# Moving weight-term work, constant loads and an input load between chunks of a time-mix and GELU kernel

## Chip, cores and metric

The kernel runs on one core of one Trainium2 chip. The metric is the device time of one execution in microseconds (us). Before the change the median of three runs is 881.1 us (880.5 to 881.29).

## What is computed

The reference takes x of 4 x 1024 x 512 (float32). With `xn = layernorm(x)` it computes

```
xs  = xn one step earlier in time (the first step takes the second)
k   = (xn + (xs - xn) * time_mix_k) @ Wk.T       # 704 columns
r   = (xn + (xs - xn) * time_mix_r) @ Wr.T
s_t = s_(t-1) * exp(-exp(time_decay)) + relu(k_t)
a   = layernorm((s * r) @ Wv.T) * gamma + beta
d   = gelu(f16(xn) @ W0.T + bias0)               # 2048 columns, rounded to f16
e   = f16(d @ W1.T + bias1)
out = x + a + e
```

## The kernel before

**Tiling.** The 4096 tokens are eight blocks of 512 (`TB`). A block is done in 16 chunks (`for n in range(NN)`, line 964), one for each 128 of the 2048 inner columns of the feed-forward part. Chunk n issues the up product of chunk n+2 (`up`, L790, tile `pd`; from chunk 14 on that of the next block), then the down product of chunk n (`down`, L812, into four PSUM banks `pe`), then at most one piece of the time-mix part, which has tokens in the free dimension: a product for k or r in the early chunks, output products (`out_piece`: `out_full` L686 with `out_halves` L698, or `out_three_pass`) in chunks 12 to 15. What follows a piece (its eviction, the scan) is a generator run in the next chunk.

**Exactness by terms.** Weights and inputs are split into terms, which the products add up. W0 and W1 are split in two (`split`, lines 168 to 170: ScalarE casts the high term `hi`, VectorE subtracts). W1's terms, tile `w`, are made from a raw load `w1raw` in block 0, stored to DRAM and loaded from there in later blocks; it has two buffers, so that the split of chunk n+2 comes after the down product of chunk n. For k and r block 0 uses raw float32 weights in slow float32 products (`raw_k`, `raw_r`, L387; the last 64 hidden columns in `raw_halves`, tile `pkr`, L604); later blocks use `three_pass` with three terms for each weight tile (k or r, h of 0 to 4): L630 with two terms into bank `pa`, L387 with the third into bank `pb`, then ScalarE evicts `a` (L642) and VectorE adds `y` (L643). Each of those ten weight tiles gets its terms in `split_kr` (line 238): on VectorE a mask `wu` (L235), a difference `wd` (L243) and the third term (L247), on ScalarE two casts (L245, L246), and three stores to DRAM put on the list `stores`. `fetch_kr` (line 883) calls `load_kr`, three loads of 256 KB, for a later use. The tag `kr` has six buffers, two sets of terms.

**Order.** All instructions of TensorE, VectorE, ScalarE and SyncE inside the loop are in an order written out by hand (`manual_schedule`): each engine runs its own in this order and waits for semaphores. In a chunk the order is: up product, gelu of it (L800) and a cast (L805), down product, W1 load of later blocks (`load_w1`, L221), the piece's products, in block 0 the next raw W1 load (L208), then the jobs that `put(n, ...)` has hung on chunk n, in the order of the puts, woven with what follows the last piece; at the end, in block 0, the split of W1 for chunk n+2, and `store_weights`, which empties `stores` (L204). All loads and stores in the loop go through the one SP queue.

**Background jobs that the change touches.**
- `split_kr` in block 0: k's tile h in chunk 1 + 2h, r's in chunks 1, 3, 5, 7, 11.
- `load_late_constants` (lines 155 to 164) in chunk 4 of block 0: five loads of 256 KB and two of 128 KB for `wvraw` (the value weights, first used by `out_full` in chunk 12) and three broadcast loads (gamma, beta, bias1).
- In block 1: `fetch_x` (`load_x` of block 2, four loads) in chunk 2; its statistics (`stats`, L305 and L306) in chunks 4 and 5, `norm_apply` (L309) in chunk 6, and 16 transposes (`turn`, L331) in chunks 6 to 9 as 1, 6, 6, 3. `store_w0l` of group g in chunk 2g (four stores of 256 KB each); `split_wv` (three terms of `wvraw`, for blocks 2 on) of tile h in chunks 9, 11, 11, 12, 13, 13; r's `fetch_kr` for h of 2 to 4 in chunks 7 to 9.

**Buffers.** Products of the time-mix part and `pd` share four PSUM banks in turn (`ps_mm`). Tiles named by `temp` share six buffers. The tag `x` has one buffer: the x of the next block, and `xres`, in which the block's output is summed up and from which it is stored (`finish`, L775, store at L779; in the first two chunks of the block after). Most 128x512 tiles share 62 buffers of the tag `q`.

## Time and profile before

| | |
|---|---|
| median of three runs | 881.1 us (880.5 to 881.29) |
| the profiled execution: time, span | 882.43 us, 880.6 us |
| granted TensorE clock, mean | 0.991 |
| busy, share of the span | TensorE 98%, VectorE 76%, ScalarE 49%, GpSimd 8% |
| chain that ended last, by engine | TensorE 93%, DMA 3%, VectorE 3%, issue 1% |
| DMA | 198.95 MB, 226 GB/s over the span |
| block 0 of the profiled execution | first down product at 40.54 us, last chunk's at 134.16 us |
| block 1 | first down product at 143.33 us |

The profile is of one execution. PE is TensorE's matmuls, PEld its weight loads, DVE VectorE, ACT ScalarE, POOL GpSimd, SP SyncE; SPq is SP's queue of DMA issues. A timeline row holds start, duration, engine, line, operation, output and inputs without their numbers, and in brackets the idle time before it and what ended that. A row of waits holds total, number and longest. A row of stretches holds the stretch, its length, each engine's busy time with the number of instructions, the granted TensorE clock (1.00 is full), the share of time that the DMA engines were busy, and GB/s. L170 is line 170 of the kernel.

### The profile page before, as it was taken

Reading aid. Unit: us, or ns where it says so; the run is one execution under the profiler, and the core shown is the slowest. Engines: PE = TensorE matmul, PEld = TensorE weight load, DVE = VectorE, ACT = ScalarE, POOL = GpSimd, SP = SyncE. Lnnn points to the kernel's source line nnn. Section 1 sums busy time; section 2 is a strip of 40 time slices with the busy share of each in tenths; the row PEclk is TensorE's granted clock in tenths of the full one; section 3 lists DMA queues with packets and bytes.
Section 4 is the critical chain, followed back from the end, with each engine's and each line's share of the span. In section 5 each row is a group of like instructions: output and inputs, shape, how many; then the busy total and the mean of one; then the engine's idle time right before and its main releaser. Section 6 shows DMA issues by size and latency. Waiting matters only on the chain.

```text
span 880.6 us, 11149 instructions
## 1 busy us (share of the span) xinstructions
PE 863.9 (98%) x3760; PEld 688.5 (78%) x3760; DVE 670.4 (76%) x1098; ACT 431.9 (49%) x733; POOL 73.9 (8%) x142
## 2 busy tenths in 40 slices
PE   8999899999999999999999999999999999999996
PEld 7676557888578888888888888888888888888885
DVE  4777986687868878779786788878886887864547
ACT  3855662437525465344644447344553446444430
POOL 1100000000002002000011000200011200200001
PEclk8999999999999999999999999999999999999998
DMA  8579874985559565776559675595656956577631
GB/s 261 207 249 331 298 256 136 339 269 187 160 184 326 203 211 173 254 270 228 178 179 313 217 248 187 178 329 202 220 192 217 310 208 222 175 242 270 235 123 49
DMA packets 102325, 198.95 MB, mean 226 GB/s; under 512 B 11231, under 2 KB 25596, under 8 KB 102268
## 3 DMA queue, kind: packets, MB, share of 16 engines
q1 hardware_dynamic: 102208, 198.22, 67.0%
q8 instruction: 30, 0.49, 0.2%
q14 instruction: 27, 0.22, 0.1%
q10 hardware_dynamic: 60, 0.02, 0.0%
HBM read 169.36 MB, written 28.84 MB: 225 GB/s over the span
## 4 chain that ended last, share of the span: by engine, by line
PE 93%; DMA 3%; DVE 3%; issue 1%; SPq 0%; ACT 0%; DVEq 0%; ACTq 0%
PE pd L790 25%; PE pe L812 24%; PE pa L630 14%; PE pb L387 7%; PE oa L727 6%; PE po L686 4%; PE ob L735 3%; PE ph L659 3%; PE pk L387 2%; PE ob L737 1%; DMA w0raw<-in_L_ffn_W 1%; PE pr L387 1%; DMA wvraw<-in_L_attn_Wv 1%; PE pkr L604 0%; PE po L698 0%
## 5 line engine op out<-in xcount | busy, mean ns | idle before, releaser
L812 PE MATMUL pe<-w,d 128*128 128x512 f32 x1008 | 250.5, 391 | 4.9 <-DVE w L170 3.1
L812 PEld LDWEIGHTS pe<-w,d 128*128 128x128 f32 x1008 | 189.5, 188 | 45.6 <-DVE w L170 4.0
L790 PE MATMUL pd<-xf,w0h 128*128 128x512 f32 x512 | 203.5, 398 | 0.0
L790 PE MATMUL pd<-xf,w0l 128*128 128x512 f32 x512 | 199.3, 389 | 0.0
L800 ACT ACTIVATE d<-pd,late_sb 128x512 f16<-128x512 f32 x128 | 87.9, 687 | 161.7 <-PE pd L790 161.4
L790 PEld LDWEIGHTS pd<-xf,w0h 128*128 128x128 f32 x512 | 96.1, 188 | 25.9 <-issue 4.9
L790 PEld LDWEIGHTS pd<-xf,w0l 128*128 128x128 f32 x512 | 96.1, 188 | 21.7 <-issue 1.9
L643 DVE SCALAR_TENSOR_TENSOR y<-pb,a 128x512 f32<-128x512 f32 x70 | 48.4, 691 | 75.3 <-PE pb L387 74.4
L642 ACT ACTIVATE a<-pa 128x512 f32<-128x512 f32 x70 | 42.0, 600 | 91.1 <-PE pa L630 91.1
L805 ACT CAST d<-d 128x512 fp32r<-128x512 f16 x128 | 79.5, 621 | 4.1
L331 DVE STREAM_TRANSPOSE xnT<-x 32x512 f32<-32x512 f32 x112 | 78.6, 702 | 2.1
L630 PE MATMUL pa<-hk,kr 128*128 128x512 f32 x140 | 54.5, 389 | 0.0
L630 PE MATMUL pa<-lk,kr 128*128 128x512 f32 x140 | 54.5, 389 | 0.0
L630 PE MATMUL pa<-hr,kr 128*128 128x512 f32 x140 | 54.5, 389 | 0.0
L630 PE MATMUL pa<-lr,kr 128*128 128x512 f32 x140 | 54.5, 389 | 0.0
L299 POOL TENSOR_SCALAR ry<-mvy 128x1 f32<-128x1 f32 x32 | 16.5, 516 | 438.2 <-DVE mvy L306 438.2
L727 PE MATMUL oa<-wv,hg 128*128 128x512 f32 x120 | 46.7, 389 | 0.0
L727 PE MATMUL oa<-wv,lg 128*128 128x512 f32 x120 | 46.7, 389 | 0.0
L645 ACT ACTIVATE y<-y 128x512 f32<-128x512 f32 x35 | 22.2, 633 | 39.7 <-DVE y L643 39.7
L387 PE MATMUL pb<-mk,kr 128*128 128x512 f32 x140 | 37.4, 389 | 0.0
L387 PE MATMUL pb<-mr,kr 128*128 128x512 f32 x140 | 37.4, 389 | 0.0
L686 PE MATMUL po<-wvraw,g 128*128 128x512 f32 x80 | 35.6, 592 | 0.0
(160 smaller groups left out, 1312.4 us busy)
## 6 DMA issues: line engine op xcount, KB each, us to landing
w<-w1d SPq DMA_DIRECT2D x110, 512.0 KB, 3.6
kr<-krd SPq DMA_DIRECT2D x210, 256.0 KB, 4.8
w0l<-w0d SPq DMA_DIRECT2D x96, 256.0 KB, 4.0
x<-in_L_attn_x SPq DMA_DIRECT2D x32, 256.0 KB, 5.8
w1d<-w SPq DMA_DIRECT2D x16, 512.0 KB, 3.4
xres<-in_L_attn_x SPq DMA_DIRECT2D x32, 256.0 KB, 5.2
krd<-wt SPq DMA_DIRECT2D x30, 256.0 KB, 4.6
out<-xres SPq DMA_DIRECT2D x28, 256.0 KB, 4.9
```

The costliest lines, as they stand in the source:

```text
L331: nc.vector.transpose(dst[i * Q : (i + 1) * Q, :, :, j, :], src[j * Q : (j + 1) * Q, :, :, i, :],)
L387: return nc.tensor.matmul(dst, w[:, c, :], src, start=(c == 0), stop=(c == NC - 1))
L630: nc.tensor.matmul(pa, w[p][:, c, :], xs[j, c][p], start=(c == 0 and p == 0), stop=(c == NC - 1 and p == 1),)
L642: nc.scalar.activation(a, pa, AF.Copy, scale=1.0 + 1.0 / S)
L643: nc.vector.scalar_tensor_tensor(y, pb, -1.0 / S, a, ALU.mult, ALU.add)
L659: nc.tensor.matmul(pa, w[:, c].rearrange("p two k -> p (two k)"), xs[j, c][p], start=(c == 0 and p == 0), stop=(c == NC - 1 and p == 1),)
L686: nc.tensor.matmul(pos[s], gs[i, h][:, s * P : (s + 1) * P], wv_raw[h], start=(h == 0), stop=False,)
L727: nc.tensor.matmul(pa, gs[i, h][p][:, cols], wv[h][p], start=(h == 0 and p == 0), stop=(h == NF - 1 and p == 1),)
L790: nc.tensor.matmul(pd, w, xf[c], start=(c == 0 and p == 0), stop=(c == NC - 1 and p == 1),)
L800: nc.scalar.activation(d16, pd, AF.Gelu, bias=b0_sb[:, n : n + 1])
L805: nc.scalar.copy(d, d16)
L812: nc.tensor.matmul(pe[s] if sum_ is None else sum_, d[:, s * P : (s + 1) * P], w1[p][:, cols], start=(n == first and p == 0), stop=(n == e ...
```

## The change

In block 0, `split_kr` runs for k's five tiles in chunks 0, 1, 3, 5, 7 and for r's tiles 0 and 1 in chunks 0 and 7. The constants' loads stand in chunk 9. The splits of r's tiles 2, 3 and 4 stand in block 1, in chunks 8, 9 and 10, where `fetch_kr` calls `split_kr` if the raw weight is still there; the terms are used from SBUF in the chunk after, in place of being loaded, and are stored for later blocks. In block 1, x of block 2 is loaded in chunk 1, its statistics stand in chunks 2 and 3, its normalization in chunk 4, the transposes in chunks 6 to 9 as 4, 6, 4, 2. `store_w0l` of group g stands in chunk 4g, `split_wv` in chunks 11, 12, 13, 13, 13, 15. TensorE's instructions stay the same in number and order.

```diff
-    def split_kr(kind, h):
+    def split_kr(block, kind, h):
...
             def fetch_kr(block, kind, h):
-                ks[block, kind, h] = load_kr(block, kind, h)
+                fetch = split_kr if (kind, h) in raw_w else load_kr
+                ks[block, kind, h] = fetch(block, kind, h)
...
+                put(0, several, split_kr, (1, 0, 0), (1, 1, 0))
                 put(0, several, split_w0, (1, 2), (1, 3))
...
-                for h in range(NF):
-                    put(1 + 2 * h, split_kr, 0, h)
-                    put((1, 3, 5, 7, 11)[h], split_kr, 1, h)
+                for n, *which in ((1, 0, 1), (3, 0, 2), (5, 0, 3), (7, 0, 4), (7, 1, 1)):
+                    put(n, split_kr, 1, *which)
...
-                put(4, load_late_constants)
+                put(9, load_late_constants)
...
                     if k > 1:
-                        put(k - 2 + 2 * (k > 6), fetch_kr, i, kind, h)
+                        split_here = (kind, h) in raw_w
+                        put(k - 2 + 2 * (k > 6) + split_here, fetch_kr, i, kind, h)
...
-                    put(2, fetch_x)
+                    put(1 if i == 1 else 2, fetch_x)
                     for s in range(NS):
-                        put(4 + s // 2 if i == 1 else 4, stats, s)
-                    put(6 if i == 1 else 5, lambda: norm_apply(j, state["x"]))
-                    turns = (1, 6, 6, 3) if i == 1 else (4, 5, 4, 3)
+                        put(2 + s // 2 if i == 1 else 4, stats, s)
+                    put(4 if i == 1 else 5, lambda: norm_apply(j, state["x"]))
+                    turns = (4, 6, 4, 2) if i == 1 else (4, 5, 4, 3)
...
                 for g in range(NN // G):
-                    put(2 * g, store_w0l, g)
-                for h, n in enumerate((9, 11, 11, 12, 13, 13)):
+                    put(4 * g, store_w0l, g)
+                for h, n in enumerate((11, 12, 13, 13, 13, 15)):
                     put(n, split_wv, h)
```

## Prediction

> **What bounds the kernel now.** I read the page's first two parts, then the waits of TensorE, then the timeline of each engine where TensorE stands still. TensorE is busy for 863.9 of 880.6 us, so a change can win only the gaps. After the first 40 us there are three, all in front of the down product (L812), and all for one thing: the split second weight, `w`.

> ```profile
> PE 863.9 (98%) x3760; PEld 688.5 (78%) x3760; DVE 670.4 (76%) x1098; ACT 431.9 (49%) x733; POOL 73.9 (8%) x142
> ...
> PE pe L812 <- DVE w L170: 3.1, 2, 2.4
> PE pe L812 <- ACT w L169: 1.9, 1, 1.9
> ```

> The timeline of TensorE places them in the first block: in chunk 7 (down product due at 76.53, goes on at 77.40) and in chunk 9 (due at 88.01, first matmul at 90.03, second at 92.88).

> ```profile
> 76.30 0.39 PE L812 MATMUL pe<-w,d 128*128 128x512 f32 x1
> 77.40 1.89 PE L812 MATMUL pe<-w,d 128*128 128x512 f32 x7 [0.71 <-DVE w L170]
> 79.13 0.59 PE L387 MATMUL pr<-xr,wr 128*128 128x512 f32 x1
> ...
> 90.03 0.50 PE L812 MATMUL pe<-w,d 128*128 128x512 f32 x1 [1.85 <-ACT w L169]
> 92.88 2.86 PE L812 MATMUL pe<-w,d 128*128 128x512 f32 x7 [2.35 <-DVE w L170]
> ```

> The gaps cost more than their length: busy time by stretch shows the granted clock (column PEclk) down after the second one.

> ```profile
> 76.30:79.13 2.83, 2.12 (x10) 1.43 (x9) 2.73 (x4) 0.14 (x1) 0.57 (x1) 1.00 1.04 329
> 88.01:95.68 7.67, 3.47 (x10) 1.96 (x9) 7.49 (x12) 4.61 (x8) 0.00 (x0) 0.86 1.03 397
> 95.68:99.85 4.17, 4.17 (x33) 1.26 (x33) 4.03 (x7) 1.87 (x3) 0.00 (x0) 0.85 0.98 346
> ```

> Why is `w` late? ScalarE's and SyncE's timelines: ScalarE sits 5.10 us before the split of chunk 8's `w`, for a load issued at 75.25, behind ten constants' loads on the one SP queue (67.66 to 73.96). VectorE, late in its turn, then still does two weight splits and five transposes ahead of chunk 9's `w` (84.84 to 92.13).

> ```profile
> 67.66 2.38 SPq L159 DMA_DIRECT2D wvraw<-in_L_attn_Wv  x5
> 70.08 1.21 SPq L161 DMA_DIRECT2D wvraw<-in_L_attn_Wv  x2
> 75.25 0.33 SPq L208 DMA_DIRECT2D w1raw<-in_L_ffn_W  x1
> ...
> 81.53 0.62 ACT L169 CAST w<-w1raw 128x512 fp32r<-128x512 f32 x1 [5.10 <-DMA w1raw<-in_L_ffn_W]
> ...
> 88.54 3.57 DVE L331 STREAM_TRANSPOSE xnT<-x 32x512 f32<-32x512 f32 x5
> 92.13 0.69 DVE L170 TENSOR_TENSOR w<-w1raw,w 128x512 fp32r<-128x512 f32 x1
> ```

> [...] full clock up to 88.01, 0.86 and 0.85 in the two stretches after, 1.00 from 99.85. [...] the load that ScalarE awaited also delayed the gelu behind it (82.06), and below a wait of VectorE holds all behind it. [...] what stands behind a waiting issue waits too.

> **The change, part by part.** Times are on the old trace's clock.

> *Splits of k and r (`split_kr`).* One costs VectorE 0.46 + 0.72 + 0.61 = 1.8 us (start to start, 84.84 to 86.63), ScalarE two instructions of 0.62 and 0.63, and SP three stores of 256 KB. Chunk 0 gets two, where VectorE idles for 5.47 us (37.2 to 42.69); chunks 1, 3 and 5 keep one of two; chunk 7 keeps two; chunks 9 and 11 lose theirs; three go to the second block. In the built program's order the first two VectorE instructions of chunk 0 even move ahead of the first scans. That is 1.1 us, but the chain they lengthen ends in `w0l`, needed near 36, at about 34.4: free. ScalarE's four extra casts put chunk 1's gelu 1.9 us later (46.3 for 44.43), its result needed at 54.87: free.

> *The constants' loads leave chunk 4.* The load for chunk 8's `w` then goes out right after the store of chunk 6's, near 66.5, and lands near 71 (4.3 us for its like at 66.30, by the trace's semaphore records, from which all landings here are), long before ScalarE wants it (74.5).

> *First block, walked again.* Without the wait and with a split less in chunks 3 and 5, chunk 7's `w` leaves VectorE near 74.0, needed at 76.53: the first gap goes (79.13 - 76.30 = 2.83 us for a stretch that takes 1.82 elsewhere: 1.0 us). Chunk 8's `w` is done at 76.4, needed at 83.4. Chunk 9's is the tight one: the gelu of chunk 7 starts at 76.56 (its matmuls' end), the `w0l` behind it on VectorE ends 2.5 us later (82.06 to 84.84 less 0.28 of DMA wait), near 79.1; then the two splits and five transposes and `w` take 84.84 to 92.82 = 8.0 us: 87.1. TensorE, 1.0 us earlier, needs it at 87.2. So the second gap goes, with nothing to spare; a gap of 0 to 0.5 stays possible, and I count 0.1. What goes with it: 7.67 - 1.82 = 5.85 us up to 95.68, and in the next stretch (`pkr`) 4.17 less 4 x 0.86 = 3.44 at full clock (a float32 128x512 product takes 3.43 us for four): 0.73. Sum: 1.0 + 5.85 + 0.73 = 7.6, less 0.1.

> *The loads in chunk 9.* They stand behind chunk 10's `w1` store (VectorE near 89.5), so go out from 90.5 on. The program's waits hold the later ones to earlier landings; the seven of `wv` land by 100.6 if they take as long as in chunk 4 (10.1 us from the first issue to the last landing). The first user is chunk 12's output product, at 111.04 - 7.6 = 103.4: 3 us of cover. Behind them on SP stands the load of chunk 13's `w1`, held to about 98 and landed by 104; ScalarE comes to it near 103, TensorE at 109.6. Free, but if the cover went, each us late is a us of TensorE.

> *Three splits in the second block* (chunks 8 to 10, three stores and no load each; nine loads fewer). VectorE has the room: three transposes leave chunks 8 and 9 for chunk 6, and a `wv` split leaves chunk 9. The terms are used a chunk later; I find each done 4 us or more ahead. The `wv` splits move to chunks 11 to 15: three in chunk 13 end near 232, those ahead of the next block 4 us before their use. The `w0l` stores move from chunks 2, 4, 6 to 4, 8, 12: their old places are the stretch with DMA share 0.99 (145 to 175), so this eases it. All counted at nothing.

> *x of block 2 a chunk sooner: a new wait.* The load now stands at the end of chunk 1 and overwrites the tile whose last two output stores were issued at 154.31.

> ```profile
> 154.31 1.22 SPq L779 DMA_DIRECT2D out<-xres  x2
> 155.63 2.24 SPq L278 DMA_DIRECT2D kr<-krd  x3
> 158.03 0.32 SPq L221 DMA_DIRECT2D w<-w1d  x1
> ...
> 161.25 1.89 SPq L106 DMA_DIRECT2D x<-in_L_attn_x  x4
> ...
> 158.25 0.69 DVE L288 SCALAR_TENSOR_TENSOR mr<-lr,ur 128x512 fp32r<-128x512 f32 x1
> 160.83 0.69 DVE L643 SCALAR_TENSOR_TENSOR y<-pb,a 128x512 f32<-128x512 f32 x1 [1.89 <-PE pb L387]
> ```

> These stores landed at 160.17 and 160.82. So x goes out at 160.9, not at 158, 0.35 us sooner than before; with the least latency of its like (4.1) it lands near 165.0, with that of before (5.4) at 166.3. But its statistics moved two chunks, from 171.54 to 158.9, ahead of chunk 2's eviction `y` (160.83). VectorE thus waits some 6 us; two statistics take 1.7, `y` 0.7: it ends at 167.4 for a landing at 165.0. That `y` frees the PSUM bank which chunk 4's up product takes, at 167.07: a gap of 0.4 us, up to 1.7 for 166.3, none below 164.6. I take 0.4. Further on VectorE needs 6.0 us for each next eviction, TensorE gives 6.3: no second gap. On SP the load of chunk 4's `w` waits behind x: out at 162.9, landed by 167.5, needed at 168.88; `kr` of chunk 4 by 169.5, needed at 170.69. Both pass with 1.2 us or more.

> *Sum:* 7.6 - 0.1 - 0.4 = 7.1 us won. The profiled execution took 882.43 us (its span 880.6 and 1.8 around it): 875.3. The median of the runs shown is 881.1, 1.3 below; I take the same saving: 874.0.

> **The rivals.**
> - *VectorE keeps a gap in chunk 9 (or x lands at the slow end).* For it: 0.1 us of slack, and VectorE 98% busy in 88 to 95.7. Against it: a short gap loses no clock. Together 1 to 3 us less: 875 to 877.5.
> - *The second block's wait grows.* For it: DMA share 0.99 there, landings of 6 us and over. If x lands at 168 to 170, the gap is 3.4 to 5.4, and the clock may drop as in chunk 9 (1 to 1.5 us): 877.5 to 880.5.
> - *The saving is only moved.* The ten loads delay chunk 12's product or the `w1` loads behind them as they did in chunk 4. For it: they queue on SP again. Against it: 3 us of cover, and half the weight stores of before. It would give about 881.
> - *Slower: VectorE's wait for x in chunk 2 of the second block eats more than all.* Price: each us of landing past 164.6 is one of TensorE, and SP's `w` and `kr` behind x follow. It decides from a landing near 171 (7.1 us with 1 of clock is break-even at 170.7); 883 at 172.5. For that x must take 11 us; the longest load in this trace took 7.3.

> **How the numbers follow.** Forecast (873 to 875) 0.62; the first rival 0.22; the second 0.08; only moved 0.04; slower 0.04. The range, 872.8 to 878.0, leaves out most of the last three, and reaches below by run spread and a block-1 gap of nothing. A measurement can tell about 0.2% (1.8 us) from no change. Faster by more 0.90, within 0.05, slower 0.05.

> **What would show it.** Right: no gap of TensorE between 42 and 100, PEclk 1.00 there, ScalarE's wait for `w1raw` gone, the up product after `pkr` near 92.4 in place of 99.85, one wait of VectorE for x of 5 to 7 us in the second block with a gap under 2 us. Wrong: a gap at chunk 9 with the clock down after it, a wait of L686 for `wvraw`, or TensorE waiting for `y` again and again through the second block.

## The result, and the profile after

The changed kernel takes 874.17 us (median of 4 executions, 873.40 to 874.42), the kernel before, on the same chip, 881.19 us (4 executions, 880.50 to 881.64): the ratio is 0.992, with a 95% interval of 0.9902 to 0.9937. The forecast was 874.0 us, with a range of 872.8 to 878.0.

The profiled execution took 874.32 us. From its page:

```profile
span 872.5 us, 11125 instructions
PE 861.3 (99%) x3760; PEld 687.6 (79%) x3760; DVE 669.7 (77%) x1098; ACT 431.1 (49%) x733; POOL 73.8 (8%) x142
...
L812 PE MATMUL pe<-w,d 128*128 128x512 f32 x1008 | 248.9, 389 | 0.0
```

The down product (L812) now waits for nothing (last column: 0.0 us), and the waits of TensorE from 36 us on are an empty list. VectorE and ScalarE are as busy as before (669.7 and 431.1 us, against 670.4 and 431.9): beside nine loads of 256 KB, nothing was taken away but waiting. The timeline of TensorE shows the places where the gaps were (start, duration):

```profile
75.63 1.98 PE L812 MATMUL pe<-w,d 128*128 128x512 f32 x8
77.45 3.59 PE L387 MATMUL pr<-xr,wr 128*128 128x512 f32 x8
82.71 1.98 PE L812 MATMUL pe<-w,d 128*128 128x512 f32 x8
86.33 2.00 PE L812 MATMUL pe<-w,d 128*128 128x512 f32 x8
...
91.86 0.50 PE L790 MATMUL pd<-xf,w0h 128*128 128x512 f32 x1
```

And busy time by stretch shows the three stretches that the prediction priced, from the down product of chunk 7, from that of chunk 9, and the `pkr` products after it (stretch, length, busy PE, PEld, DVE, ACT, POOL; then PEclk, DMA share, GB/s):

```profile
75.63:77.45 1.82, 1.82 (x10) 1.50 (x8) 0.46 (x1) 1.52 (x3) 0.00 (x0) 1.00 1.00 279
86.33:88.14 1.81, 1.81 (x9) 1.26 (x7) 1.78 (x4) 1.31 (x2) 0.00 (x0) 1.00 0.53 210
88.14:91.86 3.72, 3.72 (x33) 1.13 (x33) 3.62 (x6) 0.62 (x1) 0.00 (x0) 1.00 0.90 274
```

They were 2.83, 7.67 and 4.17 us long, with the clock at 0.86 and 0.85 in the last two. Now they are 1.82, 1.81 and 3.72 at full clock: 1.01 + 5.86 + 0.45 = 7.3 us.

The spans differ by 8.1 us, the medians by 7.0. A part of that is the start. Ahead of the first down product of the first block TensorE has the same instructions in every kernel here (VectorE's order differs a little), yet that product starts at 40.54 us in the profile of before, at 39.91 in that of after, and between 38.88 and 40.54 in all profiles of this study. From it to the end, the kernel before takes 880.6 - 40.54 = 840.06 us and the changed one 872.5 - 39.91 = 832.59: the change is worth 7.47 us by one profile of each. Below I call this the span from the first down product; it compares single profiles to about 0.1 us (three profiles of one kernel gave 835.16, 835.08 and 835.05), where whole executions scatter by 1 us and more.

### The profile page after: what moved, and what is told of

Read it like the earlier page. It is cut to its first block, busy times and chain, and to the rows that moved or that the text cites. A ratio compares the mean times of both kernels' runs of the same rounds, so it can differ in the third digit from the quotient of the medians.

```text
span 872.5 us, 11125 instructions
## 1 busy us (share of the span) xinstructions
PE 861.3 (99%) x3760; PEld 687.6 (79%) x3760; DVE 669.7 (77%) x1098; ACT 431.1 (49%) x733; POOL 73.8 (8%) x142
## 4 chain that ended last, share of the span: by engine, by line
PE 97%; DVE 1%; DMA 1%; issue 0%; SPq 0%; ACTq 0%; ACT 0%; DVEq 0%
PE pd L790 27%; PE pe L812 26%; PE pa L630 15%; PE pb L387 7%; PE oa L727 6%; PE po L686 4%; PE ob L735 3%; PE ph L659 3%; PE pk L387 2%; PE pr L387 2%; PE ob L737 1%; DMA wk<-in_L_attn_Wk 1%; PE po L698 0%; PE pkr L604 0%; DVE xres L775 0%; PE pt L429 0%
## 5 line engine op out<-in xcount | busy, mean ns | idle before, releaser
L812 PE MATMUL pe<-w,d 128*128 128x512 f32 x1008 | 248.9, 389 | 0.0
L812 PEld LDWEIGHTS pe<-w,d 128*128 128x128 f32 x1008 | 189.1, 188 | 39.5
L643 DVE SCALAR_TENSOR_TENSOR y<-pb,a 128x512 f32<-128x512 f32 x70 | 48.4, 691 | 70.5 <-PE pb L387 69.5
L331 DVE STREAM_TRANSPOSE xnT<-x 32x512 f32<-32x512 f32 x112 | 78.6, 702 | 2.1
L630 PE MATMUL pa<-hr,kr 128*128 128x512 f32 x128 | 49.8, 389 | 0.0
L630 PE MATMUL pa<-lr,kr 128*128 128x512 f32 x128 | 49.8, 389 | 0.0
L387 PE MATMUL pb<-mk,kr 128*128 128x512 f32 x140 | 37.4, 389 | 0.0
L686 PE MATMUL po<-wvraw,g 128*128 128x512 f32 x80 | 35.6, 592 | 0.0
L387 PE MATMUL pb<-mr,kr 128*128 128x512 f32 x128 | 34.2, 389 | 0.0
```

Source lines behind the costliest of these rows:

```text
L331: nc.vector.transpose(dst[i * Q : (i + 1) * Q, :, :, j, :], src[j * Q : (j + 1) * Q, :, :, i, :],)
L387: return nc.tensor.matmul(dst, w[:, c, :], src, start=(c == 0), stop=(c == NC - 1))
L630: nc.tensor.matmul(pa, w[p][:, c, :], xs[j, c][p], start=(c == 0 and p == 0), stop=(c == NC - 1 and p == 1),)
L643: nc.vector.scalar_tensor_tensor(y, pb, -1.0 / S, a, ALU.mult, ALU.add)
L686: nc.tensor.matmul(pos[s], gs[i, h][:, s * P : (s + 1) * P], wv_raw[h], start=(h == 0), stop=False,)
L812: nc.tensor.matmul(pe[s] if sum_ is None else sum_, d[:, s * P : (s + 1) * P], w1[p][:, cols], start=(n == first and p == 0), stop=(n == e ...
```

## The experiments

All are edits of one of the two kernels. The ratio is to the kernel before on the same chip (medians of 881.2 to 881.6 us; 881.83 beside the single execution); where a kernel was run more than once it is that of the first run. The last column is from one profile per run.

| kernel | median us | ratio to before, 95% | span from the first down product |
|---|---|---|---|
| before | 881.19 | 1 | 840.06 |
| changed | 874.17 | 0.9902 to 0.9937 | 832.59 |
| before, constants' loads in chunk 9 | 875.07 | 0.9918 to 0.9942 | 833.85 |
| changed, constants' loads in chunk 4 | 878.37; 878.09; 876.99 | 0.9947 to 0.9975 | 835.16; 835.08; 835.05 |
| the same, k's stores of chunks 1, 3, 5 twice | 893.58 | 1.0129 to 1.0156 | 852.47 |
| the same, 9 more stores to spare memory | 882.40 | 1.0008 to 1.0025 | 839.89 |
| changed, x of the second block as before | 874.28 | 0.9905 to 0.9930 | 832.61 |
| changed, a split from chunk 5 to 7 | 875.99 | 0.9927 to 0.9950 | 834.31 |
| changed, two splits from 3 and 5 to 7 | 878.39 | 0.9962 to 0.9982 | 836.29 |
| changed, a split from chunk 7 to 8 | 873.88 | 0.9902 to 0.9929 | 832.58 |
| changed, constants' loads in chunk 11 | 875.47 | 0.9924 to 0.9948 | 834.68 |
| changed, x loaded twice | 884.09 | 1.0024 to 1.0050 | 843.32 |

**The constants' loads alone.**

```diff
-                put(4, load_late_constants)
+                put(9, load_late_constants)
```

> The kernel before, with the constants' loads in chunk 9 and nothing else changed. Theory (the constants' loads made the second gap, the crowded splits the first): the gap of chunk 9 and its lower clock go, 5.85 + 0.73 us; the gap of 1.0 us in chunk 7 stays, since VectorE still makes two pairs of splits in chunks 3 and 5. 881.2 - 6.6 = 874.6, up to 875.2 with the whole change at 874.2. ScalarE has no wait for chunk 8's w1raw. Rival (the splits hold VectorE as much as the loads do): with two splits in each of chunks 3, 5 and 7 a gap of 1 to 3 us stays in chunk 9 and the clock drops after it: 877 to 879.

Measured: 875.07 us, as the theory had it. TensorE's only wait from 36 us on is the first gap, in its timeline:

```profile
76.32 1.89 PE L812 MATMUL pe<-w,d 128*128 128x512 f32 x7 [0.71 <-DVE w L170]
```

The stretch from this down product's first matmul (75.22) to `pr` (78.04) takes 2.82 us, as in the kernel before (2.83) and not 1.82: the first gap is the splits', 1.0 us, and the move of ten loads alone wins 6.2 us. In chunk 9 there is no gap, although chunks 3, 5 and 9 have all their splits.

**The other half: constants back in chunk 4, the splits as changed.**

```diff
-                put(9, load_late_constants)
+                put(4, load_late_constants)
```

> The changed kernel, with the constants' loads back in chunk 4. Theory: chunk 8's w1raw lands near 81 again, VectorE makes chunk 9's w near 92, TensorE comes to it near 86.5 to 87; the gap of chunk 9 is then as long as before or up to 1 us longer, since the gap gained in chunk 7 is lost again there: 880.5 to 881.2. Rival (it was the splits): the gap of chunk 9 is mostly gone and the time is 875 to 877.

Measured: 878.37 us (seven executions), between the theory and its rival. The timeline of TensorE and the stretches from chunk 9's down product on:

```profile
88.13 1.88 PE L812 MATMUL pe<-w,d 128*128 128x512 f32 x7 [2.27 <-DVE w L170]
```

```profile
85.47:90.00 4.53, 2.26 (x13) 1.30 (x13) 4.44 (x7) 2.21 (x4) 0.00 (x0) 1.00 0.69 264
90.00:93.53 3.53, 3.53 (x33) 1.06 (x32) 3.43 (x6) 0.62 (x1) 0.00 (x0) 1.00 0.89 283
```

A gap of 2.3 us is left, and no lost clock. The first gap is gone with the splits alone. My theory failed in one point: I had the load of chunk 8's `w1raw` land as late as in the kernel before. By the semaphore records it is issued 32.1 us after the first down product and lands at 37.9; in the kernel before these are 34.7 and 40.9. Chunks 1 and 3 now have one split each in place of two. So three stores fewer in each stand ahead of the constants on SP (the six stores of chunk 0 go out long before). Or it is VectorE, which does one split less before it makes the `w` whose store stands ahead of them too. The next two runs ask which.

**Stores in place of splits: a first try that asked something else.**

```diff
-            stores.append((kr_dram[kind, h][p].bitcast(F32), terms[p].bitcast(F32)))
+            for _ in range(2 if kind == 0 and 1 <= h <= 3 else 1):
+                stores.append((kr_dram[kind, h][p].bitcast(F32), terms[p].bitcast(F32)))
```

> The kernel with the constants' loads back in chunk 4 (878.4 us, a gap of 2.3 us in its profile), with the three stores of k's terms of chunks 1, 3 and 5 issued twice, so that SP has as many stores ahead of the constants as in the kernel before. Theory (without r's splits in chunks 1 and 3 there are three stores less ahead of the constants' loads, which is why that kernel won 3 us that were not expected): the constants go out 1.6 us later, chunk 8's w1raw lands 1.6 to 3 us later, the gap grows by as much and the clock drops always: 880 to 882. Rival (it was VectorE's time that was won, not SP's): 878.4.

Measured: 893.58 us, far above both. SP's timeline tells why:

```profile
50.94 7.79 SPq L204 DMA_DIRECT2D krd<-wt  x6
58.83 0.38 SPq L204 DMA_DIRECT2D w1d<-w  x1
```

A second store to the same place waited for the first to land: the first was issued at 50.94 and landed at 52.95, the second went out at 52.97. From the first of six stores to the store behind them SP thus took 7.9 us instead of 3.8 (51.21 to 54.97 in the kernel before), and everything behind them in the queue waited, as the prediction had it for a waiting issue. It shows what one on SP costs; it does not answer the question.

**As many stores in chunks 1, 3 and 5 as before, to memory that nobody reads.**

```diff
+    spare = {
+        h: [dram.tile([P, TB], F32R, name=f"spare_{h}_{p}") for p in range(3)]
+        for h in range(1, 4)
+    }
...
             stores.append((kr_dram[kind, h][p].bitcast(F32), terms[p].bitcast(F32)))
+            if kind == 0 and 1 <= h <= 3:
+                stores.append((spare[h][p].bitcast(F32), terms[p].bitcast(F32)))
```

> The kernel with the constants' loads back in chunk 4, and with the terms of k's splits of chunks 1, 3 and 5 also stored to spare memory that nobody reads: three stores more per split, as many as r's splits added there in the kernel before, but no work for VectorE and no store that waits for another. Theory (r's stores ahead of the constants on SP, not r's splits on VectorE, made chunk 8's w1raw so late): it goes out 1.6 us or more later than without them, lands 1.6 to 3 us later, the gap in chunk 9 grows from 2.3 to 4 or 5 us, with the lower clock after it: 880 to 882. Rival (VectorE's time): the same as without the spare stores, 878.4.

Measured: 882.40 us, as the theory had it. With three more stores each in chunks 1, 3 and 5, and no work for VectorE, chunk 8's `w1raw` is issued 34.7 us after the first down product and lands at 40.6: where it was in the kernel before. Both waits of the second gap are back:

```profile
88.24 0.50 PE L818 MATMUL pe<-w,d 128*128 128x512 f32 x1 [1.75 <-ACT w L169]
91.64 3.35 PE L818 MATMUL pe<-w,d 128*128 128x512 f32 x7 [2.90 <-DVE w L170]
```

and so is the span: 839.89 us from the first down product, 840.06 in the kernel before (without the first gap here, so the second costs more). So more stores on SP are enough to bring the second gap back.

That does not make them its cause in the kernel before. The constants stand on SP behind the store of chunk 6's `w`. VectorE's timeline has the making of this `w`, SP's its store, first in the kernel before, then in this run:

```profile
64.83 0.69 DVE L170 TENSOR_TENSOR w<-w1raw,w 128x512 fp32r<-128x512 f32 x1 [0.48 <-ACT w L169]
65.55 0.32 SPq L204 DMA_DIRECT2D w1d<-w  x1
```

```profile
61.87 0.69 DVE L170 TENSOR_TENSOR w<-w1raw,w 128x512 fp32r<-128x512 f32 x1 [0.48 <-ACT w L169]
64.46 0.56 SPq L204 DMA_DIRECT2D w1d<-w  x1
```

In the kernel before the store goes out 0.03 us after `w` is made (65.52), and SP had been free since 65.13: what it waited for last was the work of the second split of chunk 3 on VectorE and ScalarE. In the kernel with the constants back in chunk 4 it is the same (made at 61.69, stored at 61.72), but 2.3 us sooner from the first down product, with one split of 1.8 us less in chunk 3. In the run with spare stores `w` is made as early (62.56), and SP comes to its store only 1.9 us later. So each of the two delays is enough, and my theory, that the stores and not VectorE had made the load so late, is not borne out: in the kernel before, the splits' work came last. No run has that work without its stores, so their shares are not parted. (The spare stores also move 2.4 MB more.)

**Two groups of times.** The kernel with the constants back in chunk 4 was run twice more.

> The kernel with the constants' loads back in chunk 4, once more. Its seven times lay in two groups, 876.0 to 876.6 and 878.4 to 879.9, and the profiled execution, in the lower one, had a gap of 2.3 us and a clock of 1.00 after it. Theory (a gap of that size takes the clock in some executions and not in others): two groups again, some 3 us apart; where the profiled one is in the upper group, its gap is about the same and the clock is at half for 3 to 4 us after it. Rival (the load lands late in some executions): in the upper group the gap is 4 us or more.

> The kernel with the constants' loads back in chunk 4, a third time, for a profile of its upper group (876.0 to 876.9 and 878.1 to 879.9 in twelve times; both profiles so far are of the lower one, with gaps of 2.3 and 2.2 us and full clock after them). Theory (the clock is lost in some executions): if it takes 878 or more, the gap is again about 2.3 us and the granted clock is at half for some 5 to 7 us, worth 2 to 3 us. Rival (a later landing): the gap is 4 us or more, at full clock.

Measured: 878.09 us (five executions) and 876.99 (one). All thirteen, with the mean granted clock of each:

```
876.0 .995  876.0 .995  876.0 .995  876.6 .995  876.9 .997  877.0 .997
878.1 .996  878.4 .991  878.6 .991  878.8 .991  879.1 .991  879.2 .992  879.9 .994
```

Two groups again, 2.5 us apart in the mean (876.4 and 878.9). But all three profiles fell into the lower one, with gaps of 2.27, 2.23 and 2.20 us and full clock. What makes the upper group stays open. A lost clock after the gap fits most of the mean clocks, not that of 878.1, and a lost clock at the start, which several of these profiles have (half clock from 8.15 to 14.98 us in the one of before, from 8.4 to 11.9 in the first of these three), lowers them as well. No profile of the upper group shows a lost clock after the gap.

**x of the second block, put back.**

```diff
-                    put(1 if i == 1 else 2, fetch_x)
+                    put(2, fetch_x)
...
-                        put(2 + s // 2 if i == 1 else 4, stats, s)
-                    put(4 if i == 1 else 5, lambda: norm_apply(j, state["x"]))
-                    turns = (4, 6, 4, 2) if i == 1 else (4, 5, 4, 3)
+                        put(4 + s // 2 if i == 1 else 4, stats, s)
+                    put(6 if i == 1 else 5, lambda: norm_apply(j, state["x"]))
+                    turns = (1, 6, 6, 3) if i == 1 else (4, 5, 4, 3)
```

> The changed kernel, with the second block's x, statistics, norm and transposes in the chunks that they had before. By the prediction the sooner x costs 0.4 us (0 to 1.7): 873.8. By the trace of the changed kernel VectorE's wait for x (5.0 us) ends 0.8 us before TensorE needs the bank, so nothing is gained or lost: 874.2, within 0.3. Rival (x sooner is a part of the gain, because VectorE has more room in chunk 6 and the DMA queues less to do at 160): 875 or more.

Measured: 874.28 us and 832.61 from the first down product, against 874.17 and 832.59: nothing gained, nothing lost. This part of the change is worth 0, not -0.4.

**How much x has to spare: each load of x twice.**

```diff
             nc.sync.dma_start(xs[:, s, :], x[b, rows, :])
+            if again:
+                nc.sync.dma_start(xs[:, s, :], x[b, rows, :])
```

> The changed kernel, with each of the four loads of x for the third block (those made in chunk 1 of the second) issued twice, the same rows to the same place. Theory (VectorE's wait for x holds the eviction behind it, with 0.8 us to spare): x lands 2 to 4 us later, TensorE waits 1.5 to 3.2 us in chunk 2 of the second block: 875.7 to 877.4, and 2 more if the clock drops. Rival (the wait has room that the trace does not show): 874.2 to 874.6.

Measured: 884.09 us, above both. Again the second copy waits for the first; the four rows are ready at 156.07, 159.56, 163.00 and 166.28. VectorE's timeline, SP's, and that of TensorE:

```profile
156.09 0.69 DVE L307 BATCH_NORM_STATS2 stx<-x 128x6 f32<-128x512 f32 x1 [6.15 <-DMA x<-in_L_attn_x]
159.59 0.69 DVE L307 BATCH_NORM_STATS2 stx<-x 128x6 f32<-128x512 f32 x1 [2.58 <-DMA x<-in_L_attn_x]
160.41 0.67 DVE L645 SCALAR_TENSOR_TENSOR y<-pb,a 128x512 f32<-128x512 f32 x1
```

```profile
163.67 0.33 SPq L108 DMA_DIRECT2D x<-in_L_attn_x  x1
164.05 0.43 SPq L223 DMA_DIRECT2D w<-w1d  x1
```

```profile
161.14 0.50 PE L792 MATMUL pd<-xf,w0h 128*128 128x512 f32 x1 [3.07 <-DVE y L645]
168.03 3.78 PE L814 MATMUL pe<-w,d 128*128 128x512 f32 x8 [4.01 <-DMA w<-w1d]
```

The first wait is the one expected: 3.1 us, since the statistics of a late row hold the eviction `y` behind them (it starts at 160.41, right after the statistics of the second row, for which VectorE had waited 2.58 us). The second I had left out: the load of chunk 4's `w` stands behind x on SP, goes out at 164.05 in place of 154.95 in the changed kernel, and costs 4.0 us. With a clock at half for 10.2 us (162.3 to 172.5), 4.0 of them idle anyway, that is 3.1 + 4.0 + 3.1 = 10.2 of the 10.7 us by which its span from the first down product grew. So the order that the change writes has little to spare, and is safe only while x lands about as soon as it does here.

**One split more ahead of chunk 9's `w`.**

```diff
-(5, 0, 3), (7, 0, 4)
+(7, 0, 3), (7, 0, 4)
```

> The changed kernel, with one of k's splits moved from chunk 5 to chunk 7 (three in chunk 7). Theory (no slack ahead of chunk 9's w: 0.2 us): w comes 1.8 us later and TensorE waits 1.6 us in chunk 9, without loss of clock: 874.2 + 1.6 = 875.8. Rival A (a gap of this size costs the clock too): 876.5 to 877.5. Rival B (VectorE has hidden room): 874.2.

Measured: 875.99 us, 1.7 us more from the first down product, and this gap in TensorE's timeline:

```profile
88.61 1.66 PE L812 MATMUL pe<-w,d 128*128 128x512 f32 x6 [1.50 <-DVE w L170]
```

The clock is at 1.00 after it, as it is after the gap of 0.71 us in chunk 7 of the kernel before. One split is 1.8 us of VectorE, of which 1.5 to 1.7 are TensorE's: there was no slack to speak of, as the prediction said ("nothing to spare").

**Two splits more.**

```diff
-(3, 0, 2), (5, 0, 3), (7, 0, 4)
+(7, 0, 2), (7, 0, 3), (7, 0, 4)
```

> The changed kernel, with two of k's splits moved to chunk 7, from chunks 3 and 5 (four splits in chunk 7). The run with one split moved gave 876.0, 1.8 us over 874.2, with a gap of 1.5 us and the clock at 1.00 after it. Theory: chunk 9's w comes 3.6 us later than in the changed kernel, TensorE waits 3.4 us, and a gap as long as that also takes the clock, some 4 us at half of it, so 2 us more: 874.2 + 3.4 + 2 = 879.6. Rival (only the length of the gap counts): 877.6.

Measured: 878.39 us (nine executions, 877.04 to 881.03), between the two. The profiled one (877.58 us) has this gap, and full clock after it:

```profile
89.79 1.85 PE L812 MATMUL pe<-w,d 128*128 128x512 f32 x7 [3.43 <-DVE w L170]
```

So 3.4 us of idle TensorE did not take the clock here, where 3.1 us did in the run with x twice. The length of a gap alone did not decide it; what did is not shown (last section). The nine executions part by their mean clock: five of 877.0 to 878.4 us have 0.997 or 0.998, four of 878.7 to 881.0 have 0.990 to 0.995. A clock lost in some of them would put the median between theory and rival; the one profile is of the first five and cannot show it.

**One split less there.**

```diff
-(7, 1, 1))
+(8, 1, 1))
```

> The changed kernel, with r's split of chunk 7 moved to chunk 8, so that chunk 9's w leaves VectorE 1.8 us sooner, with 2 us to spare in place of 0.2; the next w's come 1.8 us later, needed 5 us after they are made. Theory (no time is lost at that place in the changed kernel): 874.2, within 0.3. Rival (with 0.2 us to spare some executions lose a little there): 873.5 to 873.9, and a narrower spread.

Measured: 873.88 us (873.75 to 874.43) and 832.58 from the first down product: the same as the changed kernel within what can be told. It leaves 2.0 us of slack in chunk 9 (`w` is made at 84.09 and taken at 86.07) at no price that shows, but is not a faster version. No run beat the changed kernel.

**The constants' loads later.**

```diff
-                put(9, load_late_constants)
+                put(11, load_late_constants)
```

> The changed kernel, with the constants' loads in chunk 11. Theory (3 to 4 us of cover in chunk 9): the first load goes out at about 99.5 and the seven of wv land from 103.3 to 109; TensorE comes to chunk 12's output product at 102.9 and waits 4 to 5 us in it, with or without 2 us of clock: 878.2 to 881.2. Rival (wv is not needed as early, or the loads land faster with less beside them): 874.2 to 875.

Measured: 875.47 us. TensorE waits three times for a moment; the first and the last of these in its timeline are:

```profile
104.53 1.98 PE L686 MATMUL po<-wvraw,g 128*128 128x512 f32 x4 [0.27 <-DMA wvraw<-in_L_attn_Wv]
...
108.23 1.12 PE L686 MATMUL po<-wvraw,g 128*128 128x512 f32 x2 [0.32 <-DMA wvraw<-in_L_attn_Wv]
```

From its start at 103.16 to the up product behind it at 108.79 chunk 12's product takes 5.63 us, in place of 3.88 (102.92 to 106.80) in the changed kernel: 1.75 us of the 2.1 by which the span from the first down product grew (the profile is of the slowest of five executions; the medians differ by 1.3). The theory had the place right and the size wrong. I had set the landing of the last load against the start of the product. But the product takes the five tiles of `wv` one by one, 0.78 us each, and they land not much more slowly (103.0, 104.5, 105.2, 106.7, 108.2). The fifth is wanted 3.1 us after the start, at 106.3, and is 1.9 us late; the two halves are wanted only in chunk 13.

## Why the prediction was right, step by step

**Bound and cause.** Right. With the loads moved alone, ScalarE's wait for chunk 8's `w1raw` is gone, chunk 9's gap with it, and TensorE won 6.2 us. In the changed kernel SP's timeline has this load right behind a store of `w`, with no constants ahead of it, and ScalarE's timeline has its cast without a wait:

```profile
65.53 0.33 SPq L204 DMA_DIRECT2D w1d<-w  x1
65.91 0.42 SPq L208 DMA_DIRECT2D w1raw<-in_L_ffn_W  x1
```

```profile
74.03 0.62 ACT L169 CAST w<-w1raw 128x512 fp32r<-128x512 f32 x1
```

It lands at 69.98; on this trace's clock, 0.6 us earlier than the old one, the prediction's "near 71" is 70.4.

**First gap, 1.0 us, for the splits.** Right: 1.01 us, and it stays (2.82 us for the stretch) when only the loads are moved.

**Second gap, 5.85 + 0.73, less 0.1.** Right in the sum, 5.86 + 0.45 here, and 7.47 us for all by the span from the first down product, against 7.5. "Nothing to spare" is borne out. VectorE's timeline in chunk 7, with the two splits between the first and the second line:

```profile
77.79 0.69 DVE L170 TENSOR_TENSOR w0l<-w0raw,w0h 128x512 fp32r<-128x512 f32 x1 [1.70 <-ACT w0h L169]
...
82.09 3.57 DVE L331 STREAM_TRANSPOSE xnT<-x 32x512 f32<-32x512 f32 x5
85.69 0.69 DVE L170 TENSOR_TENSOR w<-w1raw,w 128x512 fp32r<-128x512 f32 x1
```

`w` ends at 86.38, TensorE takes it with its second matmul at 86.56. The smaller term is `pkr`: 3.72 us in place of the 3.44 that four products at full clock would give.

**Which part earns it.** The prediction gave the second gap to the loads' move alone. That is one of two ways: without it, one split in place of two in chunks 1 and 3 lets the constants go out 2.6 us sooner (24.5 us after the first down product in place of 27.1), and the gap shortens to 2.3 us. Apart, the parts win 6.2 and 4.9 us by the span from the first down product, together 7.5: they are largely the same us, won twice.

**Splits in chunk 0 and in the second block.** Counted at nothing; TensorE has no wait from 36 us on, and of the 7.47 us the stretches above account for 7.3 without them. No run has them alone, nor the moved `w0l` stores and `wv` splits.

**The loads in chunk 9, "3 us of cover".** Harmless, as said, but mis-sized. SP's timeline:

```profile
89.92 2.71 SPq L159 DMA_DIRECT2D wvraw<-in_L_attn_Wv  x5
92.68 1.21 SPq L161 DMA_DIRECT2D wvraw<-in_L_attn_Wv  x2
...
96.99 0.33 SPq L208 DMA_DIRECT2D w1raw<-in_L_ffn_W  x1
```

The seven land from 93.7 to 99.4, and the product starts at 102.9: 3.5 us, as counted. But the fifth tile, the last that this product takes, lands at 98.3 and is wanted at 102.9 + 3.1 = 106.0: the cover is 7.7 us. Two chunks later the loads go out 9.3 us later, and that costs 1.75 us in the profile.

**x of the second block, a gap of 0.4.** The wait came, the gap did not. SP's, VectorE's and TensorE's timelines:

```profile
153.15 1.76 SPq L106 DMA_DIRECT2D x<-in_L_attn_x  x4
154.95 0.43 SPq L221 DMA_DIRECT2D w<-w1d  x1
```

```profile
155.95 0.69 DVE L305 BATCH_NORM_STATS2 stx<-x 128x6 f32<-128x512 f32 x1 [4.98 <-DMA x<-in_L_attn_x]
...
157.57 0.67 DVE L643 SCALAR_TENSOR_TENSOR y<-pb,a 128x512 f32<-128x512 f32 x1
```

```profile
158.03 1.07 PE L387 MATMUL pb<-mk,kr 128*128 128x512 f32 x4
158.94 0.39 PE L790 MATMUL pd<-xf,w0h 128*128 128x512 f32 x1
```

x goes out when the last output store has landed (153.13), as worked out. The term that failed is the latency: I took the least of its like, 4.1 us, and it was 2.78 (landing at 155.92). SP had issued nothing between 150.2 and 153.15; no run shows whether that is why. `y` ends at 158.24, 0.7 us before TensorE takes its bank. By the run with x twice, the price that the prediction put on each us past that point was right for VectorE (3.1 us), and too low in all: SP's `w` behind x, which it had named without a price, cost 4.0 us more.

**The median.** Predicted saving 7.1, measured 7.0 between the medians and 8.1 between the profiles: 0.6 of the latter is the start. The prediction's own profile forecast, 875.3, was 1.0 too high: 0.4 for x, 0.6 for the start. That the median came within 0.2 us is in part luck: the x term was 0.4 too dear and the `pkr` term 0.3 too large, which nearly cancel, and the four times of the changed kernel spread over 1.0 us. Of the signs named in advance all came: no gap and full clock between 42 and 100, the up product after `pkr` at 91.86 (92.4 on the old clock is 91.8 here), and one wait of VectorE for x, at 4.98 us just at the low end of "5 to 7".

## What to carry to other kernels

When a load is late, look at everything ahead of it in its queue, and at what that in its turn waits for: here ten loads stood ahead, and ahead of them the store of a `w` that a second split had made late. Taking away either gave most of the same gain. When a few per mille are at stake, measure from an event behind the start to the end of the span: it told 0.1 us from one profile, where whole times scatter by 1 us. And where a product takes a group of loads one by one, the cover is to be taken tile by tile, each landing against its own turn.

## What the runs showed of the hardware that I had not expected

```profile
86.66:90.07 3.41, 1.56 (x8) 0.98 (x6) 3.28 (x7) 1.97 (x4) 0.00 (x0) 1.00 0.92 291
90.07:93.49 3.42, 1.07 (x4) 0.66 (x5) 3.36 (x6) 3.30 (x6) 0.00 (x0) 1.00 1.06 407
93.49:96.90 3.41, 3.41 (x14) 1.80 (x16) 3.28 (x6) 1.09 (x3) 0.00 (x0) 0.50 0.98 378
```

```profile
155.45:158.86 3.41, 2.62 (x12) 1.85 (x10) 0.88 (x2) 0.00 (x0) 0.00 (x0) 1.00 0.53 147
158.86:162.28 3.42, 1.14 (x5) 0.94 (x6) 1.96 (x4) 1.16 (x2) 0.00 (x0) 1.00 0.40 152
162.28:165.69 3.41, 1.74 (x5) 0.82 (x3) 3.28 (x6) 1.78 (x4) 0.00 (x0) 0.50 0.61 169
```

In the 3.41 us right ahead of the fall TensorE was idle for 2.35 us in the kernel before, for 2.28 in the run with x twice and for 2.33 in the run with spare stores (its gap of 1.75 and the first 0.58 of that of 2.90). In the 3.41 us ahead of those, in the kernel before, it was idle for 1.85, and the clock was still full in the stretch after it. Yet a gap of 3.43 us (86.36 to 89.79, the run with four splits in chunk 7) and one of 2.27 (the constants back in chunk 4) left the clock at 1.00, in both from 80 to 100 us. Where a gap lies, and not only its length, would fit this, but that is a guess: no run was made to test it, and the ends of matmuls in a profile are modelled. In the three, TensorE was busy throughout the last 3.41 us at half clock. An estimate from these lengths: one piece costs at most 1.7 us, half of 3.41, less half of what TensorE idles in it.

**A second DMA to the same place was held on the issuing queue until the first had landed.** With the store twice the first was issued at 50.94 and landed at 52.95, and the second went out at 52.97: SP was held for 2.0 us per pair. With the load twice the second copies went out 2.8 to 3.1 us after the first. All that stood behind waited too: the store behind the six came 7.9 us after the first of them, and the load of chunk 4's `w` went out at 164.05 in place of 154.95.
